# A fixed order for the keys and values of the second attention, with work placed in the pause before it

## The chip, the cores and the metric

The kernel runs on one core of a Trainium2 chip. The metric is the device time of one execution in microseconds (us), taken as the median of several runs. Engines are named as in the profile: PE (TensorE matmul; PEld for its weight loads), DVE (VectorE), ACT (ScalarE), POOL (GpSimd) and SP (SyncE, which only issues transfers here). Each engine runs its own list of instructions in order, and they wait for each other through semaphores.

## What is computed

The reference has two layers over x (2708 rows of 256) and a 0/1 matrix adj (2708 x 2708). Each layer is a graph attention and then a mixture of eight experts with the two best used per row, both added to x:

```python
x = x + _L0_gnn_ref(_layernorm(x), adj, ...)   # q k^T attention, masked by adj, elu
x = x + _L0_ffn_ref(_layernorm(x)[None], ...)[0]   # top 2 of 8 experts, hidden 1024
x = x + _L1_gnn_ref(_layernorm(x), adj, ...)   # the attention of this case
x = x + _L1_ffn_ref(_layernorm(x)[None], ...)[0]   # top 2 of 8 experts, hidden 512
```

The second attention has scores that are a sum of a term of the row and a term of the key:

```python
H = X @ W_fc + b_fc
s_src, s_dst = H @ w_att[:d], H @ w_att[d:]
scores = where(A > 0, s_src[:, None] + s_dst[None, :] + b_att, NEG_INF)
return softmax(scores, axis=1) @ H
```

The row's term falls out of the softmax. So a key's weight is the exponential of its own term alone, and attending is a product of the mask (0 or 1) with the weighted values, divided by the sum of the weights.

## The kernel before

Rows are cut into 22 tiles of 128 (`NT`; the last has 20). Layer 0's attention and its experts come first. The experts work through slots of 128 rows; each slot ends with a scatter that adds into a DRAM tensor `xd0` (L1225). 45 slots (`OFTEN`) are always done; up to five more stand in nested conditional blocks that ask for the register `used` (L1281 to L1292). Each engine loads the register and branches for itself, and what it does first behind the blocks waits for the semaphore counts of all the others, which include the counts that a skipped block adds in place of its work.

`layer1_attention` (L602 to L778) then computes keys and values and attends. Its parts, with the names that the prediction uses:

- `normed_rows(t)` (L615): SP loads row tile t from `xd0` into `kept` (L617). `norm_stats` computes mean and variance on DVE (L207 to L209), POOL raises to the power -1/2 (L213), DVE multiplies out the deviation into `spread_of` (L215), and `normed` (L219) makes `xn` on DVE.
- `columns(t)` (L623): two transposes on PE (L225), an ACT copy into `xT` (L226), a DVE sum over `xT` into `sums_of` (L630).
- `values(t)` (L633): two PE products with `wfc` (L637, 273 columns: values, gate share, the key's term, the router's logits). ACT takes the exponential of the key's term (L643), scales the values by it into `e` (L644) and writes the logits (L645). POOL adds the bias to `kept` (L649, the kept add) and casts `e` into the first part of `parts` (L652); DVE subtracts that from `e` into the second part (L654, the subtract), so that two products of reduced precision carry the whole value.
- `key_masks` (L668) turns fp8 masks into `m` on ACT (L675), two casts for one tile of keys, `MASKS_AHEAD` = 2 tiles ahead of their use; `load_tails` (L661) does so for the last 20 keys.
- `attend(ts_, k, accs)` (L693): PE multiplies masks and parts of key tile k into six accumulators (L701, 12 products for the first group of six query tiles); the last 20 keys have L707.

Query tiles go in groups of 6, 6, 4, 3, 3. The first group does keys and values and attends on the way, with `LAG1` = 3 tiles between `values(k)` and `attend(k - 3)`; the later groups only attend. In the first group, the framework's scheduler decides the order on PE, ACT, DVE and POOL from its own costs; SP's order is as written. Matmul results of transposes and values alternate over two PSUM buffers named `misc`.

Of the kernel before, what the change touches and what calls it, by code (L numbers as in the profile page):

```python
# [9 lines left out]
F32 = mybir.dt.float32  # L10
# [17 lines left out]
NT = (N + P - 1) // P  # L28
ROWS = [min(P, N - t * P) for t in range(NT)]
# [5 lines left out]
GROUP = 4  # L35
# [4 lines left out]
VALUES = D + E  # L40
# [4 lines left out]
LAG1 = 3  # L45
# [3 lines left out]
FIRST_MASKS = 3  # L49

MASKS_AHEAD = 2


FULL_AFTER = {14: 20, 16: 24}
# [13 lines left out]
def adj_ffn_kernel(ctx: ExitStack, tc: tile.TileContext, a: dict, out: bass.AP):  # L68
    nc = tc.nc
# [9 lines left out]
    misc = ctx.enter_context(tc.tile_pool(name="misc", bufs=2, space=PSUM))  # L79
# [4 lines left out]
    ident = const.tile([P, P], F32, name="ident")  # L84
# [72 lines left out]
    wfc = const.tile([P, DC, VALUES + 1 + E], F32, name="wfc")  # L157
# [41 lines left out]
        times_gate(bfc_gate, bfc_b)  # L199


    def norm_stats(src, r, deviation=None):

        st = small.tile([P, 6], F32, name="ln_st")
        mv = small.tile([P, 2], F32, name="ln_mv")
        rs = small.tile([P, 2, 2], F32, name="ln_rs")
        nc.vector.bn_stats(st[:r], src)  # L207
        nc.vector.bn_aggr(mv[:r], st[:r])
        nc.vector.scalar_tensor_tensor(  # L209
            rs[:r, 0], once_twice[:r, 0], mv[:r, 1:2], once_twice[:r, 1],  # L210
            op0=ALU.mult, op1=ALU.add,
        )
        nc.gpsimd.tensor_tensor(rs[:r, 1], rs[:r, 0], minus_half[:r], ALU.pow)  # L213
        if deviation is not None:
            nc.vector.tensor_mul(deviation, rs[:r, 0, 0:1], rs[:r, 1, 0:1])  # L215
        return mv[:r, 0:1], rs[:r, 1, 0:1], rs[:r, 1, 1:2]

    def normed(dst, src, mean, factor):
        nc.vector.tensor_scalar(dst, src, mean, factor, op0=ALU.subtract, op1=ALU.mult)  # L219
# [80 lines left out]
    def layer0_attention(line):  # L300
        with ExitStack() as scope, ExitStack() as until_last:
# [3 lines left out]
            wide = until_last.enter_context(tc.tile_pool(name="wide0", bufs=2, side="right"))  # L305
# [44 lines left out]
                return t, src, norm_stats(src[:r], r)  # L350

            def norm_end(t, src, stats):
                r, (mean, factor, _) = ROWS[t], stats
                xn = rows.tile([P, D], F32, name="xn", bufs=4)
                normed(xn[:r], src[:r], mean, factor)
                return xn
# [18 lines left out]
            with tc.tile_pool(name="fold", bufs=1, side="right") as fold:  # L375
# [226 lines left out]
    def layer1_attention(mTs, kept, line, first_masks):  # L602
        with ExitStack() as scope:
# [8 lines left out]
            e_tail = pool.tile([P, VALUES + 1], F32, name="e_tail", bufs=1)  # L612
            sums_of = pool.tile([P, DC, NT], F32, name="sums_of", bufs=1)

            def normed_rows(t):  # L615
                r, x2 = ROWS[t], kept[:, t]
                nc.sync.dma_start(x2[:r], xd0[t * P : t * P + r, :])  # L617
                mean, factor, _ = norm_stats(x2[:r], r, spread_of[:r, t : t + 1])
                xn = rows.tile([P, D], F32, name="xn", bufs=4)
                normed(xn[:r], x2[:r], mean, factor)  # L620
                return xn

            def columns(t, xn):  # L623
                r = ROWS[t]
                xT = pool.tile([P, DC, P], F32, name="xT")
                if t < NT - 1:
                    to_columns(xT[:, :, :r], xn[:r], r)
                else:
                    tail_columns(xT, xn)
                nc.vector.tensor_reduce(sums_of[:, :, t], xT[:, :, :r], AX.X, ALU.add)  # L630
                return xT

            def values(t, xT):  # L633
                r = P
                ps = misc.tile([P, GROUP, P], F32, name="misc").rearrange("p g n -> p (g n)")
                for c in range(DC):
                    nc.tensor.matmul(  # L637
                        ps[:r, : VALUES + 1 + E], xT[:, c, :r], wfc[:, c, :],
                        start=(c == 0), stop=(c == DC - 1),
                    )  # L640
                e = e_tail if t == NT - 1 else pool.tile([P, VALUES + 1], F32, name="e", bufs=3)
                q, weight = ROWS[t], e[:r, VALUES : VALUES + 1]
                nc.scalar.activation(weight, ps[:r, VALUES : VALUES + 1], AF.Exp)  # L643
                nc.scalar.activation(e[:r, :VALUES], ps[:r, :VALUES], AF.Copy, scale=weight)  # L644
                nc.scalar.activation(  # L645
                    logits[:q, t], ps[:q, VALUES + 1 : VALUES + 1 + E], AF.Copy,
                    scale=spread_of[:q, t : t + 1],
                )
                nc.gpsimd.tensor_add(kept[:q, t], kept[:q, t], bfc_b[:q])  # L649
                if t == NT - 1:  # L650
                    return
                nc.gpsimd.tensor_copy(parts[:r, t, 0, : VALUES + 1], e[:r])  # L652
                with nc.allow_low_precision("what is left has twelve bits"):
                    nc.vector.tensor_tensor(  # L654
                        parts[:r, t, 1, : VALUES + 1], e[:r], parts[:r, t, 0, : VALUES + 1],
                        ALU.subtract,
                    )
# [10 lines left out]
            def key_masks(ts_, k):  # L668

                masks = {}  # L670
                for b in sorted({t // GROUP for t in ts_}):
                    here = [t for t in ts_ if t // GROUP == b]
                    q0, q1 = here[0] * P, here[-1] * P + ROWS[here[-1]]
                    m = pool.tile([P, GROUP * P], F32R, name="m", bufs=2 * (MASKS_AHEAD + 1))
                    nc.scalar.copy(m[:, : q1 - q0], mTs[b][:, k, q0 - b * BN : q1 - b * BN])  # L675
                    masks.update({t: m[:, t * P - q0 : t * P - q0 + ROWS[t]] for t in here})
                return masks

            def converted():

                queue, g0 = [], 0
                for wide in GROUPS:
                    ts_ = list(range(g0, g0 + wide))
                    for k in range(NT - 1):
                        queue.append(key_masks(ts_, k))
                        if len(queue) > MASKS_AHEAD:
                            yield queue.pop(0)
                    g0 += wide
                yield from queue

            masks_of_keys = converted()
# [37 lines left out]
                    )  # L729
                    line.add(finish(t, raw, total))  # L730

            ahead = [normed_rows(t) for t in range(2)]
            cols = columns(0, ahead.pop(0))
            g0, total, since = 0, None, 0
            for g, wide in enumerate(GROUPS):
                if g == 2:

                    assert g0 >= FIRST_MASKS * GROUP
                    first_masks.close()


                    n = FULL_AFTER[experts1.early]
                    guess = experts1.open([i * (n // RING) * E // (n + GROUP) for i in range(RING)])
                ts_ = list(range(g0, g0 + wide))
                accs = [ps_acc.tile([P, EVEN], F32, name="acc") for _ in ts_]

                every = 2 if wide < GROUP else 1
                line.gap = NT // wide // every
                for k in range(NT + (LAG1 if g == 0 else 0)):
                    if g == 0:  # L750
                        if k + 2 < NT:
                            ahead.append(normed_rows(k + 2))
                        if k < NT:
                            now = cols
                            if k + 1 < NT:
                                cols = columns(k + 1, ahead.pop(0))
                            values(k, now)
                        if k >= LAG1:
                            attend(ts_, k - LAG1, accs)
                    else:  # L760
# [57 lines left out]
    class Experts:  # L818
# [64 lines left out]
        def route(self, t, x, logits=None):  # L883
# [10 lines left out]
            mean, once, twice = norm_stats(x[:r], r)  # L894
# [490 lines left out]
```

## Time and profile before

| | us |
|---|---|
| median of 3 runs (1309.57 to 1316.13) | 1314.93 |
| profiled execution, its own time | 1303.23 |
| its span, first to last instruction | 1301.5 |
| PE busy | 1196.5 (92%) |
| DVE, ACT, POOL busy | 535.7, 439.3, 424.9 |
| last product of layer 0's experts ends | 859.48 |
| first load of `kept` (L617) issued | 866.66 |
| first transposes of the second attention | 871.52 |
| first attending product (L701) | 883.35 |
| last product of the first group (L707) ends | 942.2 |

Times in the lower half are microseconds from the start of the profiled span. The page's 40 slices are 32.5 us each. A row of the timeline has start, length, engine, line, operation, output and inputs, number of instructions and, in brackets, the idle time before it and what ended it. A float32 matmul leaves two records, so two products show as x4. A row of the windows view has, for each engine, its busy time and the number of instructions, then the granted clock (1.00 is full), the share of time in which the DMA engines were busy, and what they moved.

### The profile page before, as it was taken

How to read it: one execution, taken by the hardware profiler on the slowest of the kernel's cores; microseconds unless marked ns; L12 is line 12 of the kernel's file. 1: busy time of each engine (PE TensorE's matmuls, PEld its weight loads, DVE VectorE, ACT ScalarE, POOL GpSimd, SP SyncE). 2: the span in 40 equal slices, each digit the busy share in tenths (PEclk: the TensorE clock that was granted, in tenths of full speed). 3: DMA queues.
4: the chain of work that ended last, by engine and by line, in shares of the span. 5: the costliest groups of instructions: out<-in, count | busy, mean ns of one | idle time of the engine just before them, and what ended most of it. 6: DMA issues, size and time to landing. Idle time of an engine off the chain costs nothing. (4 is left out here: it accounts for less than half of the span.)

```text
span 1301.5 us, 20845 instructions
## 1 busy us (share of the span) xinstructions
PE 1196.5 (92%) x7074; PEld 962.8 (74%) x7074; DVE 535.7 (41%) x2087; ACT 439.3 (34%) x1281; POOL 424.9 (33%) x553
## 2 busy tenths in 40 slices
PE   7999999999999999999999999958987878999890
PEld 5776666656666665899999999947987767899880
DVE  6613833635626435532121212237464656321114
ACT  3221222212122122532323333335744447444440
POOL 4100111110110202443333333346343556555450
PEclk9999999999999999899999999978998989999995
DMA  8601365996928518175668645540004125544357
GB/s 270 219 1 66 106 178 128 256 248 199 257 73 212 122 62 318 53 204 142 214 214 279 201 125 152 166 107 3 1 26 179 38 70 171 177 136 141 125 179 260
DMA packets 107242, 197.83 MB, mean 152 GB/s; under 512 B 26753, under 2 KB 81718, under 8 KB 100986
## 3 DMA queue, kind: packets, MB, share of 16 engines
q1 hardware_dynamic: 77276, 110.09, 29.4%
q0 software_dynamic: 27040, 83.56, 20.1%
q10 hardware_dynamic: 2814, 2.77, 0.7%
q8 instruction: 59, 0.97, 0.3%
q14 instruction: 53, 0.43, 0.1%
HBM read 263.63 MB, written 66.12 MB: 253 GB/s over the span
## 5 line engine op out<-in xcount | busy, mean ns | idle before, releaser
L1191 PEld LDWEIGHTS mm<-xe,ring 128*128 128x128 f32 x2192 | 267.1, 195 | 27.6 <-issue 15.7
L1191 PE MATMUL mm<-xe,ring 128*128 128x128 f32 x2192 | 276.7, 280 | 11.1 <-issue 4.0
L1207 PE MATMUL acc<-ring,hT 128*128 128x256 f32 x1096 | 266.2, 380 | 3.5 <-ACT hT L1199 2.5
L1199 ACT ACTIVATE hT<-mm,ring 128x128 f32<-128x128 f32 x548 | 156.1, 368 | 253.8 <-issue 177.0
L1207 PEld LDWEIGHTS acc<-ring,hT 128*128 128x128 f32 x1096 | 194.7, 190 | 23.9 <-ACT hT L1199 2.9
L504 PE MATMUL acc<-v,p 128*128 128x257 f32 (+1 forms) x880 | 208.9, 389 | 0.0
L447 PE MATMUL s<-g,xnT 128*128 128x512 f32 x420 | 203.5, 599 | 3.2 <-DVE mT L459 3.2
L1213 DVE TENSOR_TENSOR y<-acc,bias 128x256 f32<-128x256 f32 x92 | 39.0, 424 | 359.7 <-PE acc L1207 356.3
L504 PEld LDWEIGHTS acc<-v,p 128*128 128x128 f32 (+1 forms) x880 | 152.9, 190 | 18.1 <-issue 0.8
L1120 POOL DMA_INDIRECT ring<-L_ffn_packed,weight_row x98 | 103.5, 1057 | 180.7 <-issue 145.1
L701 PE MATMUL acc<-parts,m 128*128 128x266 f32 x924 | 138.4, 307 | 19.0 <-ACT m L675 10.9
L701 PEld LDWEIGHTS acc<-parts,m 128*128 128x128 f32 x924 | 125.5, 198 | 26.9 <-ACT m L675 13.3
L972 POOL DMA_INDIRECT disp<-row,to x88 | 87.8, 997 | 138.3 <-DVE to L969 56.4
L213 POOL TENSOR_TENSOR ln_rs<-ln_rs,minus_half 128x2 f32<-128x2 f32 x88 | 65.3, 744 | 202.1 <-DVE ln_rs L209 179.2
L459 DVE TENSOR_SCALAR mT<-s 128x512 fp8e4<-128x512 f32 x105 | 72.0, 687 | 129.9 <-ACT p L458 129.8
L458 ACT ACTIVATE p<-s 128x512 f32<-128x512 f32 x105 | 62.2, 594 | 162.4 <-PE s L453 162.2
L447 PEld LDWEIGHTS s<-g,xnT 128*128 128x128 f32 x420 | 74.8, 190 | 49.1 <-issue 41.2
L1225 POOL DMA_INDIRECT xd<-y,xg x45 | 70.9, 1576 | 85.9 <-issue 29.2
L675 ACT CAST m<-mT 128x512 fp32r<-128x512 fp8e4 (+4 forms) x168 | 71.0, 471 | 33.5 <-PE acc L701 14.3
L453 PEld LDWEIGHTS <-apart 128*128 128x128 fp8e4 x420 | 32.3, 98 | 59.9 <-issue 59.9
L334 DVE TENSOR_SCALAR apart<-adj 128x677 fp8e4<-128x677 int32 x80 | 41.0, 513 | 50.3 <-DMA adj<-in_adj_dram 50.1
L1218 POOL DMA_INDIRECT xd<-y,xg x47 | 47.1, 1001 | 20.3 <-PE tp L1168 8.2
(223 smaller groups left out, 1131.7 us busy)
## 6 DMA issues: line engine op xcount, KB each, us to landing
adj<-in_adj_dram SPq DMA_DIRECT2D x84, 338.5 KB
L_ffn_packed<-in_L_ffn_W_dram SPq DMA_DIRECT2D x16, 1024.0 KB
xg<-disp SPq DMA_DIRECT2D x98, 129.0 KB
L_ffn_packed<-in_L_ffn_W_dram SPq DMA_DIRECT2D x16, 512.0 KB
neighbours<-mT SPq DMA_DIRECT2D x5, 1408.0 KB
mT<-neighbours SPq DMA_DIRECT2D x5, 1408.0 KB
xin<-in_x_dram SPq DMA_DIRECT2D x42, 128.0 KB
ring<-L_ffn_packed SPq DMA_DIRECT2D x4, 1154.0 KB
```

The source lines that it names most:

```text
L213: nc.gpsimd.tensor_tensor(rs[:r, 1], rs[:r, 0], minus_half[:r], ALU.pow)
L447: nc.tensor.matmul(ps[:kr, :nb], xnT[:, c, k0 : k0 + kr], g[:, c, :nb], start=(c == 0), stop=False,)
L459: nc.vector.tensor_scalar(mT[:kr, k, :], ps[:kr, :nb], -BIG / 2, None, ALU.is_gt, saturate=False,)
L504: nc.tensor.matmul(accs[j][:r], p[keys, q0 : q0 + r], v[keys, k, :], start=(k == 0), stop=(k == NT - 1),)
L675: nc.scalar.copy(m[:, : q1 - q0], mTs[b][:, k, q0 - b * BN : q1 - b * BN])
L701: nc.tensor.matmul(acc[:r], masks[t], parts[:, k, i], start=(k == 0 and i == 0), stop=False,)
L972: nc.gpsimd.indirect_dma_start(disp[:], bass.IndirectOffsetOnAxis(ap=to[:r, j : j + 1], axis=0), rows2[j][:r], None,)
L1120: nc.gpsimd.indirect_dma_start(w, None, packed[:], bass.IndirectOffsetOnAxis(ap=self.weight_row[:, s : s + 1], axis=0), bounds_check=E * P ...
L1191: nc.tensor.matmul(ps[:, i, :], w[:, c * hidden + f * P : c * hidden + (f + 1) * P], xe[:, c, :], start=(c == 0), stop=(c == DC - 1),)
L1199: nc.scalar.activation(hT[:, f, :], ps[:, i, :], AF.Gelu, bias=w[:, b1 + f : b1 + f + 1])
L1207: nc.tensor.matmul(ps, hT[:, f, :], w[:, w2 + f * D : w2 + (f + 1) * D], start=(f == 0), stop=(f == hc - 1),)
L1225: start = nc.gpsimd.indirect_dma_start(xd[:], at, y, None, bounds_check=N - 1, oob_is_err=False, compute_op=ALU.add)
```

## The change

Keys and values of the first group get a function of their own, `keys_and_values`, under `tc.manual_schedule` for PE, ACT, DVE and POOL: there these four engines take instructions in the order in which the program writes them. `normed_rows` is split into `norm_begin` (load, statistics, power) and `norm_end` (normalise, then the spread product), three and two tiles ahead of the values; `columns` is one tile ahead, `attend` two behind; the subtract (`second_part`) comes at the head of the next round, and the sum over `xT` at the end of the round. The POOL cast now stands ahead of the kept add.

Ahead of the loop stand three things: one exponential of a single column, whose result is overwritten later; `PAUSE` = 12 products of 128x128 with 128x512, float32, into a `misc` buffer that nobody reads; and the masks of two key tiles (before, the scheduler placed three there, and the tails).

```diff
+PAUSE = 12
...
-            def normed_rows(t):
+            def norm_begin(t):
                 r, x2 = ROWS[t], kept[:, t]
                 nc.sync.dma_start(x2[:r], xd0[t * P : t * P + r, :])
-                mean, factor, _ = norm_stats(x2[:r], r, spread_of[:r, t : t + 1])
+                return norm_stats(x2[:r], r)
+
+            def norm_end(t, mean, factor, _, variance):
+                r, x2 = ROWS[t], kept[:, t]
                 xn = rows.tile([P, D], F32, name="xn", bufs=4)
                 normed(xn[:r], x2[:r], mean, factor)
+                nc.vector.tensor_mul(spread_of[:r, t : t + 1], variance, factor)
                 return xn
...
-                nc.vector.tensor_reduce(sums_of[:, :, t], xT[:, :, :r], AX.X, ALU.add)
...
+                if t < NT - 1:
+                    nc.gpsimd.tensor_copy(parts[:r, t, 0, : VALUES + 1], e[:r])
                 nc.gpsimd.tensor_add(kept[:q, t], kept[:q, t], bfc_b[:q])
-                if t == NT - 1:
-                    return
-                nc.gpsimd.tensor_copy(parts[:r, t, 0, : VALUES + 1], e[:r])
+                return e
+
+            def second_part(t, e):
+                r = P
...
+                queue = [key_masks(*x) for x in todo[:MASKS_AHEAD]]
+                yield
+                for x in todo[MASKS_AHEAD:]:
+                    queue.append(key_masks(*x))
+                    yield queue.pop(0)
                 yield from queue
...
+            def keys_and_values(ts_, accs):
+                nc.scalar.activation(spread_of[:, :1], ident[:, :1], AF.Exp)
+                idle = misc.tile([P, GROUP, P], F32, name="misc").rearrange("p g n -> p (g n)")
+                for _ in range(PAUSE):
+                    nc.tensor.matmul(
+                        idle, ident, wfc.rearrange("p c n -> p (c n)")[:, : GROUP * P],
+                        start=True, stop=True,
+                    )
+                next(masks_of_keys)
+                stats, xn, xT, e = {}, {}, {}, {}
+                for i in range(-3, NT + LAG1 - 1):
+                    if 0 <= i - 1 < NT - 1:
+                        second_part(i - 1, e.pop(i - 1))
+                    if i + 3 < NT:
+                        stats[i + 3] = norm_begin(i + 3)
+                    if 0 <= i + 2 < NT:
+                        xn[i + 2] = norm_end(i + 2, *stats.pop(i + 2))
+                    if 0 <= i + 1 < NT:
+                        xT[i + 1] = columns(i + 1, xn.pop(i + 1))
+                    if 0 <= i < NT:
+                        e[i] = values(i, xT[i])
+                    if 0 <= i - 2 < NT:
+                        attend(ts_, i - 2, accs)
+                    if 0 <= i < NT:
+                        nc.vector.tensor_reduce(
+                            sums_of[:, :, i], xT.pop(i)[:, :, : ROWS[i]], AX.X, ALU.add
+                        )
...
+                if g == 0:
+                    with tc.manual_schedule(engines={
+                        mybir.EngineType.PE, mybir.EngineType.Activation,
+                        mybir.EngineType.DVE, mybir.EngineType.Pool,
+                    }):
+                        keys_and_values(ts_, accs)
```

More of the change, by code (lines that the diff above doesn't have):

```diff
@@ L199, in fold_gate, with norm_stats @@
         times_gate(bfc_gate, bfc_b)
-    def norm_stats(src, r, deviation=None):
+    def norm_stats(src, r):
         st = small.tile([P, 6], F32, name="ln_st")
@@ L213, in norm_stats @@
         nc.gpsimd.tensor_tensor(rs[:r, 1], rs[:r, 0], minus_half[:r], ALU.pow)
-        if deviation is not None:
-            nc.vector.tensor_mul(deviation, rs[:r, 0, 0:1], rs[:r, 1, 0:1])
-        return mv[:r, 0:1], rs[:r, 1, 0:1], rs[:r, 1, 1:2]
+        return mv[:r, 0:1], rs[:r, 1, 0:1], rs[:r, 1, 1:2], rs[:r, 0, 0:1]
     def normed(dst, src, mean, factor):
@@ L352, in norm_end @@
             def norm_end(t, src, stats):
-                r, (mean, factor, _) = ROWS[t], stats
+                r, (mean, factor, *_) = ROWS[t], stats
                 xn = rows.tile([P, D], F32, name="xn", bufs=4)
@@ L679, in converted @@
             def converted():
-                queue, g0 = [], 0
+                todo, g0 = [], 0
                 for wide in GROUPS:
[L683 to L687, printed above, removed]
-                    g0 += wide
+                    todo.extend((range(g0, g0 + wide), k) for k in range(NT - 1))
+                    g0 += wide
+                queue = [key_masks(*x) for x in todo[:MASKS_AHEAD]]
[3 more added lines that the diff above has]
+                    yield queue.pop(0)
                 yield from queue
@@ L730, in evict @@
                     line.add(finish(t, raw, total))
-            ahead = [normed_rows(t) for t in range(2)]
-            cols = columns(0, ahead.pop(0))
+            def keys_and_values(ts_, accs):
[25 more added lines that the diff above has]
+                        )
             g0, total, since = 0, None, 0
@@ L748, in layer1_attention @@
                 line.gap = NT // wide // every
[L749 to L760, printed above, removed]
+                if g == 0:
[4 more added lines that the diff above has]
+                        keys_and_values(ts_, accs)
+                for k in range(NT if g else 0):
+                    if g > 0:
                         if g == 2 and k % GROUP == 0:
@@ L893, in route @@
             ]
-            mean, once, twice = norm_stats(x[:r], r)
+            mean, once, twice, _ = norm_stats(x[:r], r)
             yield
```

## The prediction, on record before the changed kernel ran

> **What bounds the kernel now.** The page puts TensorE at 92% of the span, so I looked for the stretch where it is not the bound. The page's granted-clock row has two weak spots; one, near slice 27, is the start of the second attention. The windows view over that stretch (columns: window, length, busy time and instructions of PE, weight loads, DVE, ACT, POOL, granted clock, DMA share, GB/s):
>
> ```profile
> 859.50:871.50 12.00, 0.00 (x0) 0.01 (x1) 2.96 (x12) 2.98 (x8) 3.57 (x13) 0.62 0.41 97
> 871.50:894.25 22.75, 17.04 (x62) 12.64 (x62) 15.22 (x62) 8.91 (x27) 16.34 (x26) 0.68 0.27 81
> 894.25:941.10 46.85, 46.85 (x328) 43.88 (x326) 27.39 (x87) 35.26 (x105) 22.04 (x40) 1.00 0.01 1
> ```
>
> First a pause of 12 us in which TensorE does nothing, then 22.75 us of filling at a clock of 0.68, then a steady part with PE busy without a gap. Only the first two can be shortened. The timeline says why filling is slow:
>
> ```profile
> 877.33 0.49 ACT L644 ACTIVATE e<-misc,e 128x264 f32<-128x264 f32 x1
> ...
> 882.89 0.41 POOL L652 CAST parts<-e 128x265 fp32r<-128x265 f32 x1
> ...
> 883.35 2.16 PE L701 MATMUL acc<-parts,m 128*128 128x266 f32 x6 [3.54 <-POOL parts L652]
> ```
>
> The first exponentials and values (e, L644) are ready at 877.82, but POOL casts them only at 882.89, behind the powers (L213) and kept adds (L649) of later row tiles; PE waits 3.54 us for that and starts to attend at 883.35. One steady iteration, from the timeline:
>
> ```profile
> 922.29 0.38 PE L225 MATMUL misc<-ident,xn 128*128 128x128 f32 x2
> ...
> 922.51 1.09 PE L637 MATMUL misc<-wfc,xT 128*128 128x273 f32 x4
> ...
> 923.23 1.85 PE L701 MATMUL acc<-parts,m 128*128 128x266 f32 x12
> ...
> 924.92 0.38 PE L225 MATMUL misc<-ident,xn 128*128 128x128 f32 x2
> ```
>
> It recurs every 2.63 us. I split that as 0.25 for the transposes, 0.92 for the values (the chain of waits gives L637 0.92 to 0.93 per iteration), 1.46 for attending.
>
> The pause ends with layer 0's last scatter. In the chain of waits it runs from 862.67 to 866.11, and SP issues the first load of kept (L617) at 866.66.
>
> **The change, part by part.** In the instruction lists of the two built kernels, everything outside this stage stands in the same order; SP's list is unchanged.
>
> *Pipeline order.* POOL now has four powers, then cast, kept add, power for each tile. I followed the new lists by hand, each instruction starting when its engine is free and its inputs are there, with durations from the rows (statistics L207, L208, L209 0.43, 0.18 and 0.21, power 0.70, normalise 0.41, cast 0.41, subtract L654 0.43, xT copy 0.37, exponential and scale 0.19 and 0.50, logits 0.27). The same bookkeeping, fed with the old lists and the trace's clock, starts attending at 883.5 and ends at 942.1; the trace has 883.35 and 941.83. With kept(0) landing at the old 868.83 and a full clock, the new lists give: first transposes at 868.83 + 0.46 + 0.21 + 0.30 (statistics with hand-overs) + 0.72 (power) + 0.41 + 0.15 (normalise) = 871.1; the second pair, which stands ahead of the first values, at 872.4; the values at 872.7, done at 873.8 (0.92 and 0.2 of draining); exponential and scale to 874.5; first cast at 874.6, subtract at 875.1. On DVE the subtract stands ahead of tile 4's statistics and tile 3's normalise, which ends at 876.7; the fourth transposes, the third values and then the first attending matmul follow at 876.8, 877.1 and 878.1. From there TensorE has 1.46 + 18 x 2.63 + 0.92 + 2 x 1.46 + 0.74 (tail, L707) = 53.4 us: end at 931.5, a gain of 10.3.
>
> *The twelve products.* A 128x512 float32 product has the form of L447:
>
> ```profile
> 422.28 1.95 PE L447 MATMUL s<-g,xnT 128*128 128x512 f32 x4
> 424.06 0.39 PE L453 MATMUL s<-minus_big,apart 128*128 128x128 bf16 x4
> ```
>
> Two products take 424.06 - 422.28 = 1.78 us, so 0.89 each. The built list places nine of the twelve ahead of the branch on `used`, directly behind the last product of layer 0 (ends 859.48), and three behind the branch. The nine need 8.0 us and end at 867.5. On the not-taken side PE must reach its semaphore count (the nine included) before it adds the skipped blocks' count, and SP's first load of kept waits for that sum: in the old list the count was reached at 859.5, in the new one at 867.5, after the scatter's 866.11. So SP issues at about 867.8, not 866.66: 1.1 us later (bounds: 0.5, if the semaphore is seen at once and the scatter's own 0.55 us of handling was already past; 2.5, if PE needs 1 to 2 us to fetch instructions behind its branch). Every first instruction of the other engines after the branch waits for the same count. The three products follow from about 868.2 to 870.9, before the first transposes at 872.2, so they are free; with 2 us of fetching they would end at 872.4 and cost 0.2. Gain so far 10.3 - 1.1 = 9.2.
>
> *Clock.* The clock moves on a grid of 3.41 us. Windows cut on this grid (PE busy time, then the clock):
>
> ```profile
> 875.97:879.39 3.42, 2.96 (x8) 0.50 0.68 211
> 879.39:882.80 3.41, 0.42 (x3) 1.00 0.00 0
> 882.80:886.21 3.41, 2.77 (x8) 0.50 0.00 0
> ...
> 968.13:971.55 3.42, 1.66 (x14) 1.00 0.01 2
> 971.55:974.96 3.41, 3.41 (x17) 0.50 0.22 78
> ...
> 1012.51:1015.92 3.41, 2.14 (x18) 1.00 0.14 44
> 1015.92:1019.33 3.41, 2.80 (x22) 1.00 0.00 0
> ...
> 1067.12:1070.53 3.41, 2.25 (x14) 1.00 0.00 1
> 1070.53:1073.94 3.41, 3.41 (x17) 0.50 0.23 76
> ```
>
> At full clock a window with 1.66 busy is followed by half speed, one with 2.14 is not, one with 2.25 is: the border is near 2.1 to 2.25 of 3.41. At half clock 2.77 does not lift it, 2.96 does. In the new fill, between 872.2 and 879.3 (first transposes to first attending matmul), PE has four pairs of transposes and three of values, 4 x 0.38 + 3 x 0.92 = 4.3 us of work in 7.1 us, 2.1 per window (1.8 with the transposes at 0.25): at the border or below it. So the products carry the full clock only to about 872; it probably falls once and needs a full window to rise. Stepping the grid's phase through the bookkeeping, with these borders, leaves gains from 4.0 to 9.2, most between 5 and 8. A fully busy slow window loses 1.7 us; part of it lies in waits. I take 2.2 us. Gain: 9.2 - 2.2 = 7.0.
>
> The row that bears on a rule here is the one with 2.25 us of work, after which the clock still fell. The Trainium skill ("TensorE: Matmul & The Clock Gate", Part 1) says that the clock falls after an idle window of about 3.4 us and advises against gaps over some 3 us; no gap of the new fill is so long, so by the rule the clock would hold and the gain be 9.2; the rows speak for less, and the sum keeps 7.0.
>
> *Edits at nothing.* The table load (1.28 us at 874.53) ran beside the first values (874.44 to 876.60); moved into the pause, together with two sets of masks in place of three and without the tails (2.58 and 0.49 us before), ACT is done near 871.4, ahead of the first copy near 872.8; without that cover it would cost up to 1.3. The masks of the third tile (0.93) and the tails (0.49) now come inside the loop, where ACT has 0.5 us free per iteration. The spread product and the sum over xT change places on DVE and keep their count; DVE's iteration is 1.8 to 2.2 us, under 2.63. Behind 942 nothing changes order, so the rest moves along.
>
> **Sum.** Profiled execution 1303.23 - 7.0 = 1296.2 (span near 1294.5). That execution lies 11.7 us below the median of the runs, 1314.93; I take the same microseconds from the median: **1307.9 us**.
>
> **Rivals.**
> *The fill runs slow* (no gain that can be told): the clock falls early, as the rows with 1.66 and 2.25 allow, and stays down for three or four windows: the worst phases leave a gain of 4.0, 1310.9. With the issue delay at 2.5 as well, 2.6: 1312.3.
>
> *A new loop becomes the bound* (slower). In the fixed order, subtract(i-1), statistics(i+3), power(i+3), cast(i), subtract(i) form a circle between DVE and POOL. Its length from the rows: 0.33 + 0.46 + 0.21 + 0.36 + 0.67 + 0.44 = 2.47 us, and 2.58 with a longer hand-over at each step: only 0.05 to 0.16 under the 2.63 of PE. Each 0.1 us above 2.63 costs 20 x 0.1 = 2 us; from 2.98 on, a gain of 7.0 is gone. If the power takes its longest, 1.19 in place of 0.70 (the spread in L213's rows), and the subtract its longest, 0.95 in place of 0.43, the loop is 3.48 and the loss 17: 1325. Against it: the median power is 0.701 us and the cast's longest 0.458. For it: DVE and POOL now wait for each other in every iteration, which the old order avoided by letting them run apart.
>
> *The pause products hold the clock* (better than the forecast): 9.2, or 10.3 if the nine cost no delay: 1304.6 to 1305.7. For it: nothing idles longer than 1.5 us.
>
> **How the numbers follow.** Forecast (gain 4.5 to 8.5) 0.50; clock held, 0.20; slow fill 0.18; loop 0.12. The range takes the better rival and the slow fill, plus 2 to 3 us because the three runs themselves spread over 6.6: 1301.5 to 1313.5. A half per cent, about what a measurement of this kernel can tell from no change, is 6.6 us and cuts through the forecast: 0.35 of its 0.50 fall on the faster side, with the 0.20 of the clock held: 0.55. Same: 0.15 + 0.18 = 0.33, and the loop's 0.12 as slower.
>
> **What would show it.** Right: the first cast near 876 instead of 882.89, the first attending matmul between 879 and 882 instead of 883.35; the first kept load near 867.8; iterations at 2.63 from about 885; the tail ending near 935. Wrong: iterations longer than 2.7 with PE waiting for the cast or the subtract (loop); kept loads issued at 866.7 (the nine do not delay); a clock of 1.00 throughout (gain 9 or more); or a change behind 942.

## Result and the profile after

No difference that can be measured: 1314.88 us (median of 20 runs, 1309.76 to 1319.85) against 1316.02 us for the kernel before on the same chip (20 runs, 1309.57 to 1321.57), a ratio of 0.9996 with a 95% interval of 0.998 to 1.0011. The forecast was 1307.9 us, a gain of 7.0.

The place to look is the stage from layer 0's last product to the end of the first group's last product, which the change is about. It can be cut in three: the **gate** (until SP issues the first load of `kept`), the **fill** (until the first attending product) and **attending**. The windows view of the profiled execution after, cut there (window, length, busy time and instructions of PE, weight loads, DVE, ACT, POOL, then the granted clock, DMA share, GB/s):

```profile
863.94:872.25 8.31, 8.16 (x19) 3.36 (x19) 0.78 (x2) 0.00 (x0) 1.80 (x2) 1.00 0.22 27
872.25:886.72 14.47, 10.20 (x27) 5.50 (x25) 8.32 (x28) 6.12 (x16) 6.86 (x18) 0.72 0.63 193
886.72:947.14 60.42, 57.75 (x379) 51.38 (x377) 45.38 (x130) 41.56 (x127) 33.43 (x56) 0.98 0.01 1
```

Before, the three took 7.17, 16.69 and 58.89 us, 82.75 together; after, 83.20. The forecast was 8.3 (7.17 + 1.1), 11.4 at full clock (878.1 - 866.66), 53.4 and 2.2 for the clock, 75.3 together. (From 82.75 this would be a gain of 7.45. The prediction wrote 7.0 because it took 941.83 for the old end of the tail, where DVE starts to read the first accumulator; the last product ends at 942.24.) The gate is right. The fill is 2.2 us shorter; the sum has 5.2 at full clock, 3.0 with the clock's 2.2 in it. Attending is 1.5 us longer instead of 5.5 shorter, and here PE is idle for 2.7 us (60.42 less 57.75), where before it was busy for 58.77 of 58.89.

The timeline of one steady iteration after shows who stops whom:

```profile
916.09 0.72 POOL L654 TENSOR_TENSOR kept<-kept,L_gnn_b_fc_b 128x256 f32<-128x256 f32 x1
916.16 0.94 DVE L660 TENSOR_TENSOR parts<-e,parts 128x265 fp32r<-128x265 f32 x1 [0.55 <-POOL parts L653]
...
917.02 0.41 DVE L209 BATCH_NORM_STATS2 ln_st<-kept 128x6 f32<-128x256 f32 x1
...
917.47 0.18 DVE L210 BATCH_NORM_AGGREGATE ln_mv<-ln_st 128x2 f32<-128x6 f32 x1
...
917.69 0.22 DVE L211 SCALAR_TENSOR_TENSOR ln_rs<-once_twice,ln_mv 128x2 f32<-128x2 f32 x1
...
918.06 0.74 POOL L215 TENSOR_TENSOR ln_rs<-ln_rs,minus_half 128x2 f32<-128x2 f32 x1 [1.25 <-DVE ln_rs L211]
...
918.38 0.41 PE L225 MATMUL misc<-ident,xn 128*128 128x128 f32 x2 [0.20 <-DVE xn L219]
...
918.75 0.40 POOL L653 CAST parts<-e 128x265 fp32r<-128x265 f32 x1
...
919.18 0.94 DVE L660 TENSOR_TENSOR parts<-e,parts 128x265 fp32r<-128x265 f32 x1 [0.55 <-POOL parts L653]
```

From subtract to subtract it is 3.02 us (919.18 - 916.16), and this is the circle of the loop rival: DVE waits 0.55 for POOL's cast, POOL waits 1.25 for DVE's statistics, PE waits 0.20 for DVE's normalise. Step by step it takes 0.86 + 0.45 + 0.22 + 0.37 + 0.69 + 0.43, where the prediction had 0.33 + 0.46 + 0.21 + 0.36 + 0.67 + 0.44. (The 0.45 + 0.22 are statistics and their sum, L209 to L211.) Only the first term is off, by 0.53: the subtract. The groups view gives its count, total and mean, after and then before:

```profile
L660 DVE TENSOR_TENSOR parts<-e,parts 128x265 fp32r<-128x265 f32 x21 | 19.8, 945 | 14.7 <-POOL parts L653 14.7
```

```profile
L654 DVE TENSOR_TENSOR parts<-e,parts 128x265 fp32r<-128x265 f32 x21 | 9.8, 466 | 7.3 <-POOL parts L652 7.0
```

All 21 subtracts take 0.945 us. The first one above starts 0.07 us behind a kept add of POOL, and so do the others: with the cast ahead of the kept add, the end of the cast releases both at once. The trace of before had this in two places, and one reads it only when DVE and POOL are laid side by side (the first two rows below show the opposite order, with the subtract first):

```profile
883.55 0.42 DVE L654 TENSOR_TENSOR parts<-e,parts 128x265 fp32r<-128x265 f32 x1
883.71 0.84 POOL L649 TENSOR_TENSOR kept<-kept,L_gnn_b_fc_b 128x256 f32<-128x256 f32 x1 [0.42 <-DVE xn L219]
...
888.48 0.73 POOL L649 TENSOR_TENSOR kept<-kept,L_gnn_b_fc_b 128x256 f32<-128x256 f32 x1
...
888.55 0.95 DVE L654 TENSOR_TENSOR parts<-e,parts 128x265 fp32r<-128x265 f32 x1 [0.35 <-POOL parts L652]
...
891.54 0.72 POOL L649 TENSOR_TENSOR kept<-kept,L_gnn_b_fc_b 128x256 f32<-128x256 f32 x1
...
891.92 0.64 DVE L654 TENSOR_TENSOR parts<-e,parts 128x265 fp32r<-128x265 f32 x1
```

The subtracts at 888.55 and 891.92 were the only two of 21 above 0.5 us, and the only two that started while a kept add was running. Where the subtract started first, at 883.55, it kept its 0.42, and the add took 0.84 instead of 0.72.

The products and the gate, from the timeline after:

```profile
863.77 7.89 PE L747 MATMUL misc<-wfc,ident 128*128 128x512 f32 x18
...
871.81 2.81 PE L747 MATMUL misc<-wfc,ident 128*128 128x512 f32 x6 [0.15 <-PEq L1321]
872.25 10.93 SPq L617 DMA_DIRECT2D kept<-xd  x22
```

Nine products ahead of the branch (18 records), three behind it, and the load 8.31 us behind layer 0's last product instead of 7.17. The first cast is at 881.85, 17.9 us behind that product instead of 23.4; the first attending product is only 1.1 us earlier (22.8 instead of 23.9), because the new order puts the values of two more tiles between the first cast and attending: 3.5 us in the sum (878.1 - 874.6), 4.87 at half clock in the trace (886.72 - 881.85), where before it was 0.46 (883.35 - 882.89). The windows view after, on the grid of 3.41 us:

```profile
871.71:875.13 3.42, 2.81 (x6) 1.06 (x6) 0.63 (x3) 2.74 (x6) 1.02 (x9) 1.00 0.43 135
875.13:878.54 3.41, 0.85 (x4) 0.40 (x4) 3.17 (x14) 0.92 (x4) 2.20 (x3) 1.00 0.77 231
878.54:881.95 3.41, 2.59 (x6) 1.63 (x6) 0.85 (x4) 1.03 (x5) 0.83 (x2) 0.50 0.81 256
...
885.37:888.78 3.41, 3.41 (x12) 2.94 (x13) 2.65 (x8) 1.61 (x6) 2.12 (x5) 0.50 0.00 0
```

The full clock lasts until 878.54, 3.9 us beyond the end of the products (874.62), while TensorE has little to do; then come three windows at half clock, in which the first values are made.

### The profile page after: what moved, and what is told of

The parts are those of the page before. It is cut to its first block, busy times and chain, and to the rows that moved or that the text cites. A ratio compares the mean times of both kernels' runs of the same rounds, so it can differ in the third digit from the quotient of the medians.

```text
span 1310.4 us, 20893 instructions
## 1 busy us (share of the span) xinstructions
PE 1209.5 (92%) x7098; PEld 964.8 (74%) x7098; DVE 543.6 (41%) x2087; ACT 438.4 (33%) x1282; POOL 424.3 (32%) x553
## 5 line engine op out<-in xcount | busy, mean ns | idle before, releaser
L447 PE MATMUL s<-g,xnT 128*128 128x512 f32 x420 | 206.4, 606 | 3.3 <-DVE mT L459 3.3
L708 PE MATMUL acc<-parts,m 128*128 128x266 f32 x924 | 134.6, 301 | 15.4 <-ACT m L681 10.4
L708 PEld LDWEIGHTS acc<-parts,m 128*128 128x128 f32 x924 | 121.9, 192 | 23.6 <-ACT m L681 12.3
L447 PEld LDWEIGHTS s<-g,xnT 128*128 128x128 f32 x420 | 75.3, 192 | 50.2 <-issue 41.9
L681 ACT CAST m<-mT 128x512 fp32r<-128x512 fp8e4 (+4 forms) x168 | 70.4, 471 | 16.9 <-PE acc L708 10.2
```

The lines of the kernel that those rows point to most:

```text
L447: nc.tensor.matmul(ps[:kr, :nb], xnT[:, c, k0 : k0 + kr], g[:, c, :nb], start=(c == 0), stop=False,)
L708: nc.tensor.matmul(acc[:r], masks[t], parts[:, k, i], start=(k == 0 and i == 0), stop=False,)
```

## Experiments

The theories: **A**, POOL's kept add stretches the subtract beside it, which closes the circle between DVE and POOL at 3.02 us; **B**, the circle is too long by its hand-overs alone; **C**, the gate and the clock ate the gain. The pieces of the stage in each profile and the steady period of the loop (iteration), in us, and the ratio of the medians to the kernel before on the same chip (where none is given, there is one execution alone):

| kernel | gate | fill | attending | stage | iteration | ratio (95%) |
|---|---|---|---|---|---|---|
| before | 7.17 | 16.69 | 58.89 | 82.75 | 2.63 | |
| before, second profile | 7.02 | 16.60 | 58.52 | 82.14 | | |
| after | 8.31 | 14.47 | 60.42 | 83.20 | 3.02 | 0.9996 (0.998 to 1.0011) |
| after, second profile | 8.08 | 14.39 | 60.15 | 82.62 | | 1.0011 (0.9989 to 1.0032) |
| 1 kept adds behind the loop | 7.90 | 14.51 | 54.89 | 77.30 | 2.64 | 1.0009 (0.9984 to 1.0033) |
| 2 kept add ahead of the cast | 7.89 | 14.43 | 62.58 | 84.90 | 3.20 | |
| 3 subtract behind the statistics | 7.89 | 14.47 | 56.37 | 78.73 | 2.64 | 0.9992 (0.9971 to 1.0013) |
| 4 no products | 7.27 | 14.45 | 60.09 | 81.81 | 3.02 | 1.002 (0.9997 to 1.0043) |
| 5 kept add replaced by a copy | 7.89 | 14.38 | 54.93 | 77.20 | 2.64 | |
| 6 = 3 and 4 | 7.42 | 14.25 | 55.13 | 76.80 | 2.64 | 0.9968 (0.9944 to 0.9992) |
| 6, second set | 7.33 | 12.60 | 54.39 | 74.32 | | 0.9959 (0.9933 to 0.9986) |
| 7 = 6, weight loads spread | 7.29 | 12.70 | 54.39 | 74.38 | | 0.9979 (0.9956 to 1.0002) |
| 8 = 6 and small products in the fill | 7.44 | 12.59 | 54.39 | 74.42 | 2.64 | 0.9936 (0.9912 to 0.9961) |
| 8, second set | 7.29 | 12.28 | 54.39 | 73.96 | | 0.9929 (0.9902 to 0.9955) |

**1. Kept adds behind the loop.** All else in the order of after.

```diff
-                nc.gpsimd.tensor_add(kept[:q, t], kept[:q, t], bfc_b[:q])
...
                         keys_and_values(ts_, accs)
+                        for t in range(NT):
+                            nc.gpsimd.tensor_add(kept[: ROWS[t], t], kept[: ROWS[t], t], bfc_b[: ROWS[t]])
```

> From the kernel after; the 22 kept adds are moved off POOL's round and stand together behind the loop, nothing else moves. The stage is measured from the end of layer 0's last product to the end of the first group's tail: 82.75 us before, 83.2 after. Theory A (POOL's kept add runs beside the two-input subtract and stretches it from 0.43 to 0.945, which makes the DVE-POOL circle longer than PE's work): subtract back to 0.41-0.45, iteration 2.63 (2.60-2.70) instead of 3.02, stage 77 (74-78.5), median 5 to 7 us under that of after. Theory B (the circle is too long by its hand-overs, whatever runs beside it): subtract may shorten, but the iteration stays at 2.9 or more, stage 81-83, total within 2 us. Theory C (the delayed gate and the fallen clock ate the gain): iteration as it may be, the stage moves by less than 2 us.

Measured: subtract 0.459 on average, iteration 2.64, stage 77.3: theory A to the number, and against B and C. The timeline of this kernel, one iteration:

```profile
913.51 0.41 POOL L653 CAST parts<-e 128x265 fp32r<-128x265 f32 x1
913.95 0.43 DVE L659 TENSOR_TENSOR parts<-e,parts 128x265 fp32r<-128x265 f32 x1 [0.67 <-POOL parts L653]
914.01 0.38 PE L225 MATMUL misc<-ident,xn 128*128 128x128 f32 x2
...
915.34 0.72 POOL L215 TENSOR_TENSOR ln_rs<-ln_rs,minus_half 128x2 f32<-128x2 f32 x1 [1.43 <-DVE ln_rs L211]
```

The subtract has 0.43 again, and PE's transposes carry no wait: PE is the bound. (The average holds one subtract of 0.94, the last, at 932.57, beside the first of the moved adds.) The total did not follow, and my expectation for it was wrong: the adds now stand on POOL ahead of the routing of the second group of query tiles, whose length goes from 39.3 (tail to tail, after) to 46.66. The groups view of POOL over that group names them:

```profile
L792 POOL TENSOR_TENSOR kept<-kept,L_gnn_b_fc_b 128x256 f32<-128x256 f32 x15 | 11.1, 784 | 0.0
```

The first power of that routing starts only behind the adds, at 948.79. So the 5.3 us won in the stage (against the second profile of after) are lost right behind it, to a queue that the routing needs. (The third group was shorter in this profile, 35.34 against 38.97, but it varies as much in one and the same program, as shown below.)

**2. Kept add ahead of the cast**, as the kernel before had it.

```diff
+                nc.gpsimd.tensor_add(kept[:q, t], kept[:q, t], bfc_b[:q])
                 if t < NT - 1:
                     nc.gpsimd.tensor_copy(parts[:r, t, 0, : VALUES + 1], e[:r])
-                nc.gpsimd.tensor_add(kept[:q, t], kept[:q, t], bfc_b[:q])
```

> From the kernel after; on POOL the kept add stands ahead of the cast again, as in the kernel before, all else as after. Theory A: the subtract no longer starts beside a kept add and takes 0.43, but the kept add's 0.72 now lies inside the circle (power, kept add, cast): 2.47 + 0.72 = 3.2 per iteration, stage 85.7 (84-87), which is slower than after by 2 to 3 us. If only the length of the subtract counted and no circle: 2.63 per iteration, stage 77. Theory B (hand-overs): as A or longer, and the subtract has no part in it. Theory C: stage within 1 us of 83.2.

Measured: the subtract is short, and the iteration is longer, 3.20 (914.84 - 911.64 from power to power), stage 84.90. The timeline of this kernel:

```profile
911.64 0.74 POOL L215 TENSOR_TENSOR ln_rs<-ln_rs,minus_half 128x2 f32<-128x2 f32 x1 [1.42 <-DVE ln_rs L211]
912.35 0.72 POOL L652 TENSOR_TENSOR kept<-kept,L_gnn_b_fc_b 128x256 f32<-128x256 f32 x1
913.01 0.40 POOL L654 CAST parts<-e 128x265 fp32r<-128x265 f32 x1
913.45 0.43 DVE L660 TENSOR_TENSOR parts<-e,parts 128x265 fp32r<-128x265 f32 x1 [1.24 <-POOL parts L654]
...
914.84 0.74 POOL L215 TENSOR_TENSOR ln_rs<-ln_rs,minus_half 128x2 f32<-128x2 f32 x1 [1.43 <-DVE ln_rs L211]
```

Power, kept add, cast, subtract in one chain: 2.47 + 0.72 = 3.19 was expected. So it is the circle that sets the pace, and the length of the subtract acts through it alone. In this circle the kept add costs 0.72 in the open and 0.53 hidden behind the subtract.

**3. Subtract behind the statistics.** The circle is opened; the collision stays.

```diff
-                    if 0 <= i - 1 < NT - 1:
-                        second_part(i - 1, e.pop(i - 1))
                     if i + 3 < NT:
                         stats[i + 3] = norm_begin(i + 3)
+                    if 0 <= i - 1 < NT - 1:
+                        second_part(i - 1, e.pop(i - 1))
```

> From the kernel after; on DVE the subtract of tile i-1 is issued behind the statistics of tile i+3 instead of ahead of them, nothing else moves. The power then no longer waits for the subtract: the circle is open. Theory A: iteration 2.63 (2.60-2.75) even if the subtract stays at 0.9, stage 77 (74-79), median 4 to 7 us under that of after. Theory B (hand-overs between DVE and POOL are the cost, not this circle): iteration 2.8 or more, stage above 80. Theory C: stage within 2 us of 83.2.

Measured: the timeline of this kernel,

```profile
914.36 0.94 DVE L660 TENSOR_TENSOR parts<-e,parts 128x265 fp32r<-128x265 f32 x1
914.41 0.38 PE L225 MATMUL misc<-ident,xn 128*128 128x128 f32 x2
914.97 0.89 POOL L215 TENSOR_TENSOR ln_rs<-ln_rs,minus_half 128x2 f32<-128x2 f32 x1
```

shows the subtract still at 0.94 beside the kept add, the power without a wait, and PE without one: iteration 2.64, stage 78.73. A long subtract does no harm where the power does not wait for it. With the first experiment this is A from two sides. The median (1305.68, before 1307.59) is 3.6 us under experiment 4 on the same chip, but against before it cannot be told from no change.

**4. No products** (`PAUSE = 0`).

> From the kernel after; PAUSE = 0, so the twelve products are left out, nothing else moves. Theory A: SP issues the first load of kept 7.2 us behind the last product of layer 0 instead of 8.3; the clock is at half from the start of the fill; iterations stay at 3.0; stage 82 (81-83.5), median within 2 us of after, on the lower side. Theory C (gate and clock ate the gain): if the gate is what counts, the stage falls by more than 3 us; if the products do hold the clock, the stage grows by 2 or more.

Measured: gate 7.27, so the products cost 0.6 to 1.0 there; fill 14.45, against 14.38 to 14.51 in the six profiles with the twelve products. They do not shorten the fill at all. Their clock is spent ahead of it. Of theory C the gate's 0.6 to 1.0 us is shown, and the iteration is 3.02 as expected. What the fallen clock costs does not show here, since the fill ran at half clock with the products and without them; experiment 8 has profiles where the clock came back earlier.

**5. A copy in place of the kept add**, one input from SBUF instead of two, 0.40 us instead of 0.72.

```diff
-                nc.gpsimd.tensor_add(kept[:q, t], kept[:q, t], bfc_b[:q])
+                nc.gpsimd.tensor_copy(spare[:q], kept[:q, t])
...
+            spare = pool.tile([P, D], F32, name="spare", bufs=1)
```

> From the kernel after; POOL's kept add (two inputs from SBUF, 0.72 us) is replaced by a plain copy of the same tile into a spare buffer (one input, about 0.43), so the bias is left out of kept. Which property of the POOL instruction stretches the subtract? If any POOL access beside it does (the subtract waits while POOL is busy): subtract 0.43 + 0.2 to 0.4 = 0.65-0.85, iteration 2.7-2.9. If only the two inputs of the add do: subtract 0.46 as with the kept adds behind the loop, iteration 2.64, stage 77-78. If neither, and the place alone counts: subtract 0.945 and 3.02 again.

Measured, from the timeline:

```profile
914.76 0.40 POOL L654 COPY spare<-kept 128x256 f32<-128x256 f32 x1
914.85 0.60 DVE L660 TENSOR_TENSOR parts<-e,parts 128x265 fp32r<-128x265 f32 x1 [0.54 <-POOL parts L653]
```

The subtract has 0.594 on average, between the cases: a copy with one input slows it too, by less than I expected. The subtract lasts 0.28 to 0.29 beyond the end of POOL's instruction in both kernels (915.45 - 915.16; 917.10 - 916.81). Alone it takes 0.43, so it had about a third of its work behind it when POOL ended, after 0.31 us beside the copy as after 0.65 us beside the add. What sets its length is when POOL's instruction ends; this reads as a subtract that is held until then, which the rows fit but do not prove. By the sum the circle is then 2.47 + 0.16 = 2.63. In the trace the subtracts recur every 2.67 (914.85 - 912.18) and PE's transposes every 2.64 without a wait, so the circle and PE stand level, and attending is as short as without a kept add in the loop (54.93, against 54.89).

**6. Both edits, 3 and 4.**

> From the kernel after, two edits: the subtract of tile i-1 behind the statistics of tile i+3, and PAUSE = 0. Theory A with the gate's price: 78.7 (subtract late) less 1.4 (without the products, as measured) = stage 77.3 (76.3-78), iteration 2.64, first load of kept 7.2 us behind layer 0's last product; median 3 to 6 us under before, lowest of the kernels run so far. Rival C (the products hold the clock and are worth their delay): stage 79 or more.

Measured: 1304.22 against 1307.71, 0.3% faster than before (interval 0.9944 to 0.9992), and 5.8 us under after on the same chip (1309.99). Expected stage 77.3, measured 76.80.

**Second profiles of before and after**, for a doubt of another kind: in the first traces the third group of query tiles took 35.65 us before and 38.97 after (tail to tail, from the end of one to the end of the next). Theory D: part of any gain is given back there, because one more pair of routing scatters meets the loads of the expert weights. Theory E: that group varies from execution to execution.

> The kernel before, unchanged: a second profile of it, to see what of the differences belongs to one execution. Theory A (DVE-POOL circle): stage 82.75 again (82.3-83.2), subtract median 0.43. Theory D (part of any gain is given back in the third group of query tiles, because five pairs of scatters leave POOL ahead of the end of the second group in the kernel before and only four in the kernels with the written order): second group 40.8, third group 36.1 again (tail to tail). Theory E (the third group varies from execution to execution): third group anywhere between 36 and 40, whatever the kernel.

> The kernel after, unchanged, timed beside the next two. Theory A: stage 83.2 (82.5-83.8), iteration 3.02, subtract 0.945. Theory D: second group 39.3, third group 39.4. Median within 2 us of before, and 3 to 5 us above the kernel without products and with the subtract behind the statistics.

Measured: the second profile of before has 39.40 for the second and 38.29 for the third group, where the first had 40.76 and 35.65. The same program: D as I had put it falls. Over all profiles the third group lies between 35.3 and 40.2. Behind the stage, executions of one kernel differ by several us; the stage itself repeats to 0.6 in before and in after (in kernel 6 to 2.5, for a reason that experiment 8 comes to).

**7. Weight loads spread** over the third group, on ACT's queue.

```diff
-                        if g == 2 and k % GROUP == 0:
+                        if g == 2 and k % 6 == 2:
                             next(guess, None)
...
-                nc.sync.dma_start(self.ring[i], self.packed_weights[0][e * P : (e + 1) * P, :])
+                nc.scalar.dma_start(self.ring[i], self.packed_weights[0][e * P : (e + 1) * P, :])
```

(The kernel "just named" is that of experiment 6.)

> From the kernel just named, one more edit: the four loads of expert weights (ring) at the third group of query tiles are issued on ACT's queue, one behind each sixth key tile, instead of all four by SP at once. The scheduler puts some instructions of DVE in the third group in another order because of it. Theory D: a pair of scatters then waits 4 us or less instead of 7, TensorE's hole in the third group (11 us) shrinks to under 8, third group 36 or less instead of 39.4, median 3 us or more under the kernel without this edit. Theory E: third group as before or as after, no relation; total within 2 us. Against: the weights come later, and if the experts wait for them the gain is lost at their start.

Measured: third group 40.18, median 1304.80 beside 1304.22 without the edit. POOL's longest wait for a scatter in that group is 5.3 us, against 7.0 in after and 5.9 without the edit, but its waits sum to 16.6, against 13.9 and 13.4. So the edit brings nothing, and it did not take the waits away: D's forecast (a wait of 4 us or less, a group of 36 or less) failed, but D is not tested further by it.

**8. Small products in the fill**, 128 columns each, behind the first four pairs of transposes.

```diff
                         xT[i + 1] = columns(i + 1, xn.pop(i + 1))
+                        if i < 3:
+                            nc.tensor.matmul(
+                                accs[0][:, :P], ident, wfc[:, 0, :P], start=True, stop=True
+                            )
```

> From the kernel with the subtract behind the statistics and without the twelve products: one product of 128x128 with 128 columns (about 0.22 us at full clock) behind each of the first four pairs of transposes, into an accumulator that is overwritten later; they stand where TensorE has gaps of 0.35 to 0.5 us in the fill. Theory C2 (what holds the fill back is the half clock, and it lifts as soon as a window of 3.41 us is busy almost throughout): clock back 3 to 6 us earlier, first attending product 18.5-20.5 us behind layer 0's last product instead of 21.7, stage 74-75.5, median 1 to 3 us lower. Rival (the fill is bound by the chain of DVE, POOL and ACT): first attending product within 0.5 us of 21.7, stage 76.5-77.5, and the products cost up to 1 us.

Measured: clock back 9 us behind the first load, fill 12.59, ratio 0.9936. That fits the theory, but experiment 7, which has no such products, had 12.70 too. So both were run side by side:

> The kernel with the subtract behind the statistics and without products, unchanged, timed beside the next on one chip. Theory C2 (the small products lift the clock earlier): first attending product 14.3 us behind the first load of kept, clock back to full 15 to 16 us behind that load, stage 76.8, median 1 to 3 us above the next kernel. Theory E2 (where the clock lifts is a matter of where its grid falls, with or without the small products): first attending product 12.6 or 14.3 in either, medians within 1 us.

> The kernel with the four small products in the fill, unchanged, timed beside the one without them. Theory C2: first attending product 12.6 us behind the first load of kept, clock back 9 to 11 us behind it, stage 74.4, median 1 to 3 us lower. Theory E2: as before, 12.6 or 14.3, medians within 1 us. Both: iteration 2.64, and faster than the kernel before by 0.3 to 0.7%.

Measured: 1292.03 without and 1290.14 with the small products, fill 12.60 and 12.28, clock back at 876.8 in both, 9.0 and 7.9 us behind the first load. The intervals of the two ratios overlap widely. Without them the fill was 14.25 in one profile and 12.60 and 12.70 in two, from the same order of instructions in the stage; with them 12.59 and 12.28. So it is shown that the clock can come back early without the small products; that they help is not. In the two of these three with the short fill, the window ahead of the lift had 3.06 and 3.07 us of work; in the one with the long fill the same window had 3.00, and the clock stayed. With the small products it had 3.41 and 3.37. Against the first transposes, the grid of the profile with the long fill lay 0.24 to 0.26 us from that of the two others, so where the grid falls (theory E2) is the likelier cause; it is not shown. What the earlier clock is worth can be read: about 1.6 us of fill and 0.7 of attending (14.25 and 55.13 against 12.60 and 54.39).

## Why the prediction was wrong

*The step that failed: "From there TensorE has 1.46 + 18 x 2.63 ...".* The iteration is 3.02, and attending 7.0 us longer than the sum's 53.4 (60.42). Of the 7.0, 5.5 go when the kept adds leave the loop (54.89 in experiment 1); 0.5 lies at half clock (54.89 - 54.39), and 1.0 was missing from the sum (54.39 - 53.4). The prediction drew the circle, gave it 2.47 to 2.58, and wrote that from 2.98 on a gain of 7.0 is gone: the mechanism was the loop rival's, at a chance of 0.12. What was mis-sized is one term, the subtract: 0.43, the median of its row. Its longest, 0.95, was in the rival, coupled with a power at its longest, as if both were rare. The question that was not asked is what stood beside the subtract when it took 0.95. It was the kept add, already running, and the change puts a running kept add there in every round. So the long value was not the tail of a spread but the price of the new order.

A page had a sentence for it. The Trainium skill ("GPSIMD Engine Reference", 8. Key points) says that GPSIMD shares its SBUF interfaces with VectorE and contends with VectorE instructions that have two SBUF inputs; the subtract has two. The runs agree (0.43 alone, 0.59 beside a copy, 0.945 beside the add); the section gives no price. Not every instruction of POOL counts: in the trace of before a power of two columns (884.87 to 885.57) ran beside a whole subtract that took 0.43.

*The clock.* The prediction took 2.2 us for one fall. The fall came, and lasted three windows: the fill at 14.4 is 3.0 above the sum's 11.4 at full clock (no run had full clock throughout; with the clock back 8 to 9 us behind the first load it took 12.3 to 12.7), and where PE is the bound, another 0.5 to 2.0 us of attending lie at half clock (54.89 and 56.37 in experiments 1 and 3, 54.39 at full clock). So 3.5 to 5 in place of 2.2, if all that the fill has over the sum is the clock's, which is not shown. The row ahead of the fall has 0.85 us of work in 3.41, below every border in the prediction; the estimate of 1.8 to 2.1 per window began at the first transposes, but the window that decided began 1.5 us ahead of them, in the 2.0 us of idling behind the products (874.62 to 876.64). The borders themselves came from few rows and do not hold: the kernel before also fell behind a window with 2.41 us of work (520.98 to 524.40), its second profile held behind one with 1.56 (862.80 to 866.21), and at half clock 3.04 did not lift it (881.95 to 885.37, after) where 2.96 had. The busy time of one window gives no border in these traces. The rule of the Trainium skill ("TensorE: Matmul & The Clock Gate", Part 1), a fall after an idle window of about 3.4 us, would have had the clock hold; the measurement decides against it.

*The gate.* Right: 8.31 - 7.17 = 1.14 where 1.1 was written, in the way described (nine products ahead of the branch). Over all profiles with products 7.9 to 8.3, without 7.0 to 7.4. The upper bound of 2.5 rested on 1 to 2 us of fetching behind PE's branch; no run shows it, and the first product behind the branch starts 0.15 us after the nine have ended.

*Pipeline order.* Right in its first half: the cast leaves its queue early (17.9 us instead of 23.4 behind the last product), and the fill is 2.2 us shorter with the clock against it. The full-clock sum is borne out too: attending takes 54.39 where the clock is full and the circle open, for 53.4 in the sum.

*Edits at nothing.* The table load and masks cost nothing that shows: ACT is done with them at 875.51, ahead of its first copy at 877.12. "DVE's iteration is 1.8 to 2.2 us, under 2.63" counted busy time; its waits for POOL (0.55 a round) and the stretched subtract fill the 3.02. This was the same error seen from DVE.

In sum, measured less predicted: gate 0.0, fill 0.8 (14.47 - 11.44 - 2.2), attending 7.0. That is 7.9 us, the whole difference of 83.2 and 75.3.

## What to carry to other kernels

When an order is written by hand, lay the engines side by side for one round and ask of every instruction what will now run beside it: a duration's outliers in the old trace may be the new order's normal value. A circle between two engines that stands 0.1 us under the bound has no room for one stretched instruction; open it (here by issuing the subtract three instructions later) rather than shorten it. And work placed in a pause to keep a clock up is worth only what still holds when the real work begins.

## What the hardware showed

- A 128x265 subtract on DVE with two SBUF inputs takes 0.43 us alone, 0.59 when it starts beside a running 0.40 us copy of POOL and 0.945 beside a running 0.72 us two-input add; it ends 0.28 to 0.29 us behind POOL's instruction each time. Where it started first, it kept 0.42 and the add took 0.84 (883.55, before).
- In the six profiles with the twelve products, one window of 3.41 us with 0.85 to 1.52 us of TensorE work was followed by half clock for three windows or four (10.2 us after, 13.7 in experiment 3); after's longest idle stretch before that fall was 2.02 us.
- From one execution to the next of the kernel before, the second and third groups behind the stage change by 1.4 and 2.6 us, and what lies behind the groups by 6.5; the stage read between its own two events repeats to 0.6 us in before and after and shows what the total cannot.
